# Three groups of loads move from SyncE's DMA queue to ScalarE's: the rows of the automaton, the gate's inputs, the gate's mix

## The chip, the cores and the metric

The kernel runs on one core of a Trainium2 chip. The metric is device time in microseconds, the median of several runs. One more execution was taken with the profiler; its own time stands beside its span in the table below. Engines are called as the profile calls them: PE (matrix multiplies), PEld (weight loads), DVE (vector), ACT (ScalarE), POOL (GpSimd), SP (SyncE, which only issues DMAs here). A "q" after an engine's name (SPq, ACTq) is its sequencer issuing a DMA.

## The reference, cut to what matters

The input x is 32 images of 8 channels, 256 x 256 pixels, f32. Layer 0 normalises x by groups of channels and adds to it a gated blend of two branches; layer 1 normalises again and adds a quantised 3x3 convolution.

```python
# layer 0, on n = groupnorm(x)
grid = n
for _ in range(15):                                  # branch 1: the lattice
    mapped = 3.9 * grid * (1 - grid)
    grid = 0.85 * (0.7 * mapped + 0.3 * conv3x3_depthwise(mapped)) + 0.15 * n
cml = clip(grid, 1e-4, 1 - 1e-4)
nca = sigmoid(conv1x1(relu(conv3x3(n, 8 -> 128)), 128 -> 8))      # branch 2: NCA
g = sigmoid(conv1x1(relu(conv3x3(concat(n, cml, nca), 24 -> 8)), 8 -> 8))   # the gate
x = x + g * cml + (1 - g) * nca
# layer 1
x = x + dequantised(conv3x3(quantised(groupnorm(x)), quantised(w))) + bias
```

## The kernel before

The program has a first stage that does all of layer 0 and the normalisation of layer 1, and a second stage for the quantised convolution. The change is in the first.

**Work of the first stage.** It goes through eight groups of four images. Four kinds of work are interleaved in one program:

- The lattice (`lattice`, `half`): for each group and channel, 15 steps, each in two halves of two images. A half is 32 multiplies (L502) into two of PE's result tiles, then on DVE two instructions `gt` (L513) and two that make the next state (L523). The states are `m_a` and `m_b`, two of each. Where a half writes `m_a`, `exchange` (L477, L478) issues two small DMAs on SP that copy rows of `m_a` between partitions; PE reads them in the next step of the same two images, which is two halves later. There are 896 exchanges. After every half `background` (L465) issues up to four more DMAs on SP from a list `later`: loads `d_a`, `d_b` of the next channel and stores of the finished one.
- NCA (`nca`): for each image eight tiles of 32 rows. `rows` (L569) loads the next tile into one of two buffers `im`, with 4 DMAs of 384 KB. A call of `hidden` is 12 multiplies from `im` (L588), then ACT's `h` (L596). There are eight calls to a tile, each followed later by four multiplies (L604) that sum into `acc`; after the tile, ACT's `nca` (L610).
- The gate (`gate`): again eight tiles to an image, one group behind NCA. `inputs` (L665) loads the next tile with 3 DMAs of 384 KB (two for `gin`, one for `gnc`; two buffers of each). PE's 80 multiplies L767 are followed by ACT's `r1` (L773), PE's L717 and ACT's `gate` (L719). `blend` (L675) loads `mix` with 2 DMAs of 384 KB into a single buffer, which ACT's `f` (L688) and POOL's `d` (L690) and `f` (L692) read; the next `mix` can be loaded only when these are done.
- Normalising the next group (`normalise`): loads `xr` (L306), ACT's `xq` (L370), stores (L336, L346).

**Order.** PE's order is the order of the program, written out by hand: `together` runs the lattice and lets out other work between its halves. For the other engines the planner of the framework sets the order in which their instructions are issued; each engine then issues its instructions in that order, and one that waits holds up those behind it.

**PE's result tiles.** `unit()` hands out three tiles `pt` in turn: a half takes two, a `hidden` one, a gate tile one. The multiplies that open a tile wait until its contents of three turns ago have been read, which for a `hidden` is ACT's `h`.

**DMA semaphores.** In the trace every DMA that SP or ACT issues counts on one of eight semaphores (100 to 104, 106 to 108), taken in turn across both queues, and it is issued only when the DMA that last used the semaphore has landed. SP's DMAs run on queue 1, ACT's on queue 10. In the first stage ACT issues none after its first 24 stores of zeros. In the second stage ACT issues 28 loads `yb` (L928) and 192 stores (L1001).

The lines of the loads, before the change:

```python
im = ims[(NT8 * b + t) % 2]
for k in range(2):
    for q in range(2):
        nc.sync.dma_start(im.bitcast(F32)[64 * q : 64 * q + 48, k, :, 1 : 1 + W], ...)   # L569
...
for j, to in enumerate((gin[:48], gin[48:], gnc)):
    nc.sync.dma_start(to, ...)                                                          # L665
...
for k in range(2):
    nc.sync.dma_start(mix[:, :, k, :], ...)                                             # L675
```

Of the kernel before, what the change touches and what calls it, by code (L numbers as in the profile page):

```python
# [109 lines left out]
def kernel(  # L110
# [15 lines left out]
    nc = tc.nc  # L126
# [3 lines left out]
    def dram_ap(t, offset, dims):  # L130
        return bass.AP(t.tensor, t.offset + offset, dims)
# [123 lines left out]
    with ExitStack() as one:  # L255
# [308 lines left out]
        def rows(b, t):  # L564

            im = ims[(NT8 * b + t) % 2]
            for k in range(2):
                for q in range(2):
                    nc.sync.dma_start(  # L569
                        im.bitcast(F32)[64 * q : 64 * q + 48, k, :, 1 : 1 + W],  # L570
                        dram_ap(
                            xp_s[b % NBUF], (32 * t + 16 * k + 8 * q) * ROW, [[W, 48], [ROW, 8], [1, W]]
                        ),
                    )
            return im
# [3 lines left out]
        def nca(b):  # L579
# [21 lines left out]
            def drain():  # L601
# [6 lines left out]
                if i == 3:  # L608
# [13 lines left out]
                    )  # L622

            ahead = loaded.pop(b, None) or rows(b, 0)
            for t in range(NT8):
                im = ahead
                acc = ps_a.tile([P, 512], F32, name="acc", tag="acc")
                for i in range(4):
                    hs = {}
                    for n in (i, i + 4):  # L630
                        hs[n], hs[n + 8] = hidden([im[64 * q : 64 * q + 48, :, n, :] for q in range(2)])
                        if n == 0:
                            if t < NT8 - 1:
                                ahead = rows(b, t + 1)
                            elif all((b + 1, g) in ready for g in range(4)):
                                loaded[b + 1] = rows(b + 1, 0)
                        yield 1.4
                    if i == 2 and done:
                        nc.sync.dma_start(*done)
                        done = None  # L640
                    if pend:
                        done = drain() or done
                    pend = (acc, t, i, hs)
                    yield 0.9
# [14 lines left out]
        def inputs(b, t):  # L659

            src = gs_s[b % NBUF]
            gin = gip.tile([96, 8, W], F32, name="gin", tag="gin")
            gnc = gip.tile([48, 8, W], F32, name="gnc", tag="gnc")
            for j, to in enumerate((gin[:48], gin[48:], gnc)):
                nc.sync.dma_start(  # L665
                    to, dram_ap(src, j * PART + 32 * t * C * W, [[W, 48], [4 * C * W, 8], [1, W]])
                )
            return gin, gnc

        def blend(b, t):  # L670

            src = gs_s[b % NBUF]
            mix = gip.tile([P, 3, 2, W], F32, name="mix", tag="mix", bufs=1)
            for k in range(2):
                nc.sync.dma_start(  # L675
                    mix[:, :, k, :],
                    dram_ap(src, (32 * t + 16 * k + 1) * C * W, [[W, P], [PART, 3], [1, W]]),
                )
            return mix
# [17 lines left out]
        def begin_gate(b):  # L697
            return scales(b), (inputs(b, 0), blend(b, 0))
# [9 lines left out]
        def gate(b):  # L708
# [38 lines left out]
            for t in range(NT8 + 1):  # L747
# [7 lines left out]
                if t < NT8:  # L755
                    (gin, gnc), mix = ahead
                    if t < NT8 - 1:
                        now["ahead"] = [inputs(b, t + 1)]
                    elif (b + 1) % GB:
                        staged[b + 1] = [inputs(b + 1, 0)]  # L760
                    pa = two[:, 0, :]
                    three = pa.rearrange("p (k w) -> p k w", w=W)
                    for j, src in enumerate((gin, gnc)):
                        rows_ = src.shape[0]
                        for n, (dx, to, of) in enumerate(PARTS):
                            for i in range(4):
                                T.matmul(  # L767
                                    three[32 * i : 32 * i + 32, :, to],
                                    gw[:rows_, j, dx, :], src[:, i::4, of],
                                    start=(j == 0 and n == 0), stop=(j == 1 and n == len(PARTS) - 1),  # L770
                                )
                    r1 = wk.tile([P, 512], F32, name="r1", tag="r1", bufs=1)
                    S.activation(r1, pa, AF.Relu, bias=bv[:, 0:1])  # L773
                    now["r1"], now["t"], now["mix"] = r1, t, mix
# [8 lines left out]
                def blend_(now):  # L783
                    if now["t"] < NT8 - 1:
                        now["ahead"].append(blend(b, now["t"] + 1))
                    elif (b + 1) % GB:
                        staged[b + 1] = scales(b + 1), (*staged[b + 1], blend(b + 1, 0))
# [293 lines left out]
```

## Time and profile before

| what | value |
|---|---|
| median of 3 runs | 12246.84 us (12240.68 to 12266.93) |
| the profiled execution | 12231.09 us, span 12229.3 us |
| PE busy | 10809.9 us, 88% |
| DVE busy | 7826.2 us, 64% |
| ACT busy | 3791.0 us, 31% |
| POOL busy | 1577.2 us, 13% |
| DMA on queue 1 (SP) | 1651.64 MB, 66.0% of 16 engines' span |
| DMA on queue 10 (ACT) | 89.53 MB, 2.3% |
| from 1500 to 11300 us (lattice, NCA and gate together) | PE busy 9109 of 9800 us |
| from 11660 us (second stage) | PE busy 273 of 570 us |

How to read it: the profile lists groups of instructions by source line, with the engine's idle time just before them and what ended it. "PE pt L502 <- DMA m_a<-m_a" is PE idle before a lattice multiply until the exchange of `m_a` had landed. The granted clock (PEclk) is a share of TensorE's full speed. Issuing a DMA does not count as busy time of ACT or SP, but it takes the sequencer's time, and the trace has its duration. The two rows for stretches are sums over a view of the profile that gives each engine's busy time window by window.

### The profile page before, as it was taken

The numbers are of one execution on the slowest core, as the hardware profiler recorded it, in microseconds if no ns is written. First come the engines' busy times: TensorE is split into PE (matmuls) and PEld (weight loads), VectorE is DVE, ScalarE is ACT, GpSimd is POOL, SyncE is SP. The second block draws the span as 40 slices with busy tenths as digits, with TensorE's granted clock in tenths as the row PEclk, the third lists the DMA queues.
The fourth block names the chain that finished last, engine by engine and source line by source line (L and its number), as shares of the span: only waits on it lengthen the run. The fifth ranks groups of instructions, "written<-read, shape, count | busy, mean of one in ns | idle before, by whom it ended". The sixth has DMA issues, their size and how long they took to land. (4 is left out here: it accounts for less than half of the span.)

```text
span 12229.3 us, 289998 instructions
## 1 busy us (share of the span) xinstructions
PE 10809.9 (88%) x124192; PEld 6033.0 (49%) x124192; DVE 7826.2 (64%) x11376; ACT 3791.0 (31%) x4034; POOL 1577.2 (13%) x2242
## 2 busy tenths in 40 slices
PE   4888899999999999999999999999999999999854
PEld 2544555555555555555555555555555555554222
DVE  4655666666666666666666666666666666665377
ACT  2222233332333333333333333333333333332133
POOL 1000011111111111111111111111111111111200
PEclk7999999999999999999999999999999999999776
DMA  6545567766777667766776667777677666665988
GB/s 171 97 98 102 101 136 147 143 140 138 147 142 148 137 137 145 151 141 134 148 151 139 135 140 147 143 145 149 133 146 149 141 133 129 126 123 114 204 249 259
DMA packets 2473159, 1759.74 MB, mean 144 GB/s; under 512 B 1021280, under 2 KB 2442944, under 8 KB 2471744
## 3 DMA queue, kind: packets, MB, share of 16 engines
q1 hardware_dynamic: 2380096, 1651.64, 66.0%
q10 hardware_dynamic: 91776, 89.53, 2.3%
q8 instruction: 979, 16.04, 0.6%
q14 instruction: 308, 2.52, 0.1%
HBM read 1130.62 MB, written 473.89 MB: 131 GB/s over the span
## 5 line engine op out<-in xcount | busy, mean ns | idle before, releaser
L596 ACT ACTIVATE h<-pt,bp_sb 128x1024 f32<-128x1024 f32 x2048 | 2275.6, 1113 | 4947.7 <-PE pt L588 4944.3
L588 PE MATMUL pt<-im,wp_hi 48*128 48x512 f32 x12288 | 2631.8, 424 | 165.4 <-ACT h L596 116.6
L502 PE MATMUL pt<-m_a,lw 64*64 64x325 f32 (+1 forms) x30720 | 2299.3, 433 | 464.9 <-DMA m_a<-m_a 410.1
L513 DVE SCALAR_TENSOR_TENSOR gt<-pt,d_b 128x650 f32<-128x650 f32 (+1 forms) x1920 | 1463.5, 763 | 1945.0 <-PE pt L502 1931.7
L588 PE MATMUL pt<-im,wp_lo 48*128 48x512 f32 x12288 | 2442.5, 393 | 0.2 <-issue 0.2
L513 DVE SCALAR_TENSOR_TENSOR gt<-pt,d_a 128x640 f32<-128x640 f32 (+1 forms) x1920 | 1447.2, 754 | 1531.5 <-PE pt L502 1528.2
L502 PE MATMUL pt<-m_b,lw 64*64 64x320 f32 (+1 forms) x30720 | 2200.5, 417 | 118.1 <-DVE gt L513 82.1
L502 PEld LDWEIGHTS pt<-m_a,lw 64*64 64x64 f32 x30720 | 1316.6, 138 | 1193.2 <-issue 596.9
L588 PEld LDWEIGHTS pt<-im,wp_hi 48*128 48x128 f32 x12288 | 1163.6, 185 | 1275.4 <-issue 719.4
L502 PEld LDWEIGHTS pt<-m_b,lw 64*64 64x64 f32 x30720 | 1237.4, 134 | 858.4 <-issue 463.5
L523 DVE SCALAR_TENSOR_TENSOR m_a<-gt 128x640 f32<-128x640 f32 (+1 forms) x1792 | 1431.7, 799 | 58.6
L523 DVE SCALAR_TENSOR_TENSOR m_b<-gt 128x650 f32<-128x650 f32 (+1 forms) x1792 | 1384.6, 774 | 101.3 <-DVE gt L513 2.8
L528 POOL TENSOR_TENSOR m_b<-m_b,junk 128x36 f32<-128x36 f32 x896 | 243.8, 272 | 7994.9 <-DVE m_b L523 5672.1
L588 PEld LDWEIGHTS pt<-im,wp_lo 48*128 48x128 f32 x12288 | 1168.7, 186 | 201.7 <-issue 0.6
L604 PE MATMUL acc<-h,wu_z 128*32 128x512 f32 x8192 | 1107.7, 612 | 0.0
L767 PE MATMUL pt<-gin,gw 96*32 96x384 f32 (+2 forms) x10240 | 772.0, 450 | 201.3 <-ACT gate L719 178.0
L277 PE MATMUL mark<-qw 64*64 64x1 bf16 x5760 | 947.6, 165 | 0.0
L277 PEld LDWEIGHTS <-qw 64*64 64x64 bf16 x5760 | 632.4, 110 | 205.4 <-issue 9.8
L767 PE MATMUL pt<-gnc,gw 48*32 48x126 f32 (+2 forms) x10240 | 733.1, 429 | 0.0
L767 PEld LDWEIGHTS pt<-gin,gw 96*32 96x32 f32 x10240 | 313.8, 115 | 823.7 <-issue 425.2
L690 POOL TENSOR_TENSOR d<-mix 128x256 f32<-128x256 f32 x512 | 552.1, 1095 | 1240.8 <-DVE gate L725 840.1
L767 PEld LDWEIGHTS pt<-gnc,gw 48*32 48x32 f32 x10240 | 295.0, 108 | 420.8 <-issue 415.3
(110 smaller groups left out, 5939.0 us busy)
## 6 DMA issues: line engine op xcount, KB each, us to landing
im<-xp_s SPq DMA_DIRECT2D x1024, 384.0 KB
gin<-gs_s SPq DMA_DIRECT2D x512, 384.0 KB
mix<-gs_s SPq DMA_DIRECT2D x512, 384.0 KB
gnc<-gs_s SPq DMA_DIRECT2D x256, 384.0 KB
d_a<-gs_s SPq DMA_DIRECT2D x2048, 36.0 KB
yb<-y_s ACTq DMA_DIRECT2D x28, 2432.0 KB
xr<-in_x_dram SPq DMA_DIRECT2D x128, 512.0 KB
xp_s<-hi SPq DMA_DIRECT2D x256, 256.0 KB
```

The costliest lines, as they stand in the source:

```text
L277: T.matmul(one_[dst], qw[src, 0, dst], qw[src, 0, 0:1], start=True, stop=True)
L502: T.matmul(pt[dst], lw[src, c, w, dst], rhs[src], start=first, stop=not first)
L513: V.scalar_tensor_tensor(gt.rearrange("p (u c) -> p u c", u=2), pt[:, :, : w * n], FLOOR, d[:, ts, :].rearrange("p (u t) j -> p u (t j)", ...
L523: V.scalar_tensor_tensor(to, gt, 1.0, gt, ALU.subtract, ALU.mult)
L528: G.tensor_tensor(edge, edge, junk.unsqueeze(1).to_broadcast([P, TU, 2]), ALU.mult)
L588: T.matmul(ph[:, i, :].rearrange("p (h w) -> p h w", w=W), w[64 * i : 64 * i + 48, dx, :], rhs[:, :, dx : dx + W], start=(dx == 0 and w is ...
L596: S.activation(h.rearrange("p i c -> p (i c)"), ph.rearrange("p i c -> p (i c)"), AF.Relu, bias=bp_sb)
L604: T.matmul(acc[32 * g : 32 * g + 32], wu_z[:, 24 - 8 * i : 56 - 8 * i], hs[4 * g + i], start=(i == 0), stop=(i == 3),)
L690: G.tensor_tensor(d[:, cols], mix[:, 1, k], mix[:, 2, k], ALU.subtract)
L767: T.matmul(three[32 * i : 32 * i + 32, :, to], gw[:rows_, j, dx, :], src[:, i::4, of], start=(j == 0 and n == 0), stop=(j == 1 and n == le ...
```

## The change

The three `nc.sync.dma_start` in `rows`, `inputs` and `blend` become `nc.scalar.dma_start`. They stand at the same places of the program. In all 2304 DMAs of 384 KB go from SP's queue to ACT's: 1024 for `im`, 768 for `gin` and `gnc`, 512 for `mix`.

```diff
@@ def rows(b, t):
             for k in range(2):
                 for q in range(2):
-                    nc.sync.dma_start(
+                    nc.scalar.dma_start(
                         im.bitcast(F32)[64 * q : 64 * q + 48, k, :, 1 : 1 + W],
@@ def inputs(b, t):
             for j, to in enumerate((gin[:48], gin[48:], gnc)):
-                nc.sync.dma_start(
+                nc.scalar.dma_start(
                     to, dram_ap(src, j * PART + 32 * t * C * W, [[W, 48], [4 * C * W, 8], [1, W]])
@@ def blend(b, t):
             for k in range(2):
-                nc.sync.dma_start(
+                nc.scalar.dma_start(
                     mix[:, :, k, :],
```

## The prediction

> **What bounds the kernel now.** I read the page first, then busy time by windows, then who waited for whom on PE, then single stretches of the timeline. From 1500 to 11300 us every window looks like this one (PE, PEld, DVE, ACT, POOL busy, then clock and DMA share):
>
> ```profile
> 2000.00:4000.00 2000.00, 1854.78 (x21940) 1041.44 (x21938) 1314.59 (x1963) 637.74 (x664) 287.63 (x394) 0.98 0.71 143
> ```
>
> PE is busy 93% and its order is fixed, so the first stage lasts as long as PE's work plus PE's waits. ACT is busy 32%. The longest of PE's waits in the whole run (us in total, times, longest):
>
> ```profile
> PE pt L502 <- DMA m_a<-m_a: 410.1, 153, 12.3
> PE pt L990 <- ACT ob L995: 235.6, 28, 12.8
> PE pt L767 <- ACT gate L719: 178.0, 218, 0.9
> PE pt L588 <- ACT h L596: 116.6, 84, 2.1
> ```
>
> The first is the exchange of `m_a`, an SP DMA. One case in the timeline shows why it is late:
>
> ```profile
> 2612.25 1.93 SPq L569 DMA_DIRECT2D im<-xp_s  x4
> ...
> 2614.63 0.62 SPq L477 DMA_DIRECT2D m_a<-m_a  x1
> ...
> 2615.29 0.60 SPq L478 DMA_DIRECT2D m_a<-m_a  x1
> ...
> 2626.57 1.79 PE L502 MATMUL pt<-m_a,lw 64*64 64x325 f32 x11 [8.08 <-DMA m_a<-m_a]
> ```
>
> The exchange was issued in time, but four `im` loads (1.5 MB) were ahead of it on queue 1, and it landed after them: PE waited 8.08 us. From the trace's DMA packets I worked out, for each exchange, the time from the end of L478's issue to its last packet (2112 bytes; nothing else has that size), and how many 1 KB packets queue 1 started meanwhile. The usual value is 1.0 us. In 348 exchanges over 200 such packets went first, up to 1411, and the median is then 5.4 us in the first group and 2.8 later. These 348 carry 390 of PE's 410 us. In the longest cases the packets are those of `im`, `gin` and `mix`, the transfers that move.
>
> A long wait costs twice. In the window behind this one the granted clock is 0.50:
>
> ```profile
> 2626.00:2628.00 2.00, 1.43 (x13) 0.93 (x17) 0.00 (x0) 0.00 (x0) 0.00 (x0) 0.50 1.13 342
> ```
>
> The first 11 multiplies took 1.79 us; the same group, with a warm clock, took 0.99 at 2613.64. In all PE worked 229 us at half clock next to waits for `m_a` (300 to 11300 us), half of which, 114 us, is lost.
>
> **What the change removes.** 2304 DMAs leave SP and queue 1. Two things come of it.
>
> (a) SP's time. Their issues take 521 (`im`, mean 0.509), 439 (`gin`, `gnc`, mean 0.572) and 254 us (`mix`, mean 0.496) on SP, 1.21 ms. I cost this at nothing: SP waited 3298 us for DVE to write `m_a`, and the median exchange was issued 0.06 us after that. The cover is missing in 77 exchanges issued over 0.5 us late; 87 of the 89 us that PE waited for these belong to the 348 and are counted below.
>
> (b) The queue. How soon an exchange lands when the big loads run on queue 10 beside it the first stage doesn't show. From below: as in an empty queue, 1.0 us, extra 0. From above the nearest row is the second stage, where SP's stores run beside ACT's 2.4 MB load on queue 10. A store of 112 KB lands 2.44 us after its issue when few packets of queue 10 are under way and 4.78 (median) when over 200 are: extra 2.3 us, though the load itself takes 11 to 13 us. So the other queue does not have to drain first. I put the extra latency on the 348 and compare with the moment PE wanted the data (its start less its wait): left-over waits are 33 us at 0.5, 64 at 1.0, 126 at 1.5, 248 at 2.3. I take 1.5, as an exchange has one or two packets to a DMA engine where the store has seven. Gain in waits 390 - 126 = 264; of the 114 lost to the clock some 80, since the long waits go first. Together 345 us; bounds 142 + 40 = 182 and 357 + 114 = 471.
>
> The Trainium skill speaks against this: "DMA: Bandwidth & Descriptors", section "Issuing engines are not separate DMA queues", says that DMAs of all issuers run on the same 16 engines and interleave, and that spreading them saves only issue time, by which the gain would be that of (a), nothing. The same page, section "Queues, rings and completion order", has each engine take turns between queues by packets of some 9 to 17 descriptors, which at the 46 ns of one 1 KB packet in queue 10 is an estimate of 0.4 to 0.8 us extra and a gain near 440.
>
> **What it adds: ACT issues them.** The cost of one on ACT: the second stage has the same kind on both queues, L1001 at a median of 812 ns on SP and 823 on ACT, so SP's durations can be used:
>
> ```profile
> L569 SPq DMA_DIRECT2D im<-xp_s x1024: 302/463/2093, 174.4 to 11197.1; - x171
> L665 SPq DMA_DIRECT2D gin<-gs_s x512: 302/470/1907, 1504.8 to 11639.7; - x171
> L665 SPq DMA_DIRECT2D gnc<-gs_s x256: 302/470/3036, 1505.4 to 11640.4; - x128
> L675 SPq DMA_DIRECT2D mix<-gs_s x512: 358/472/2002, 1585.7 to 11648.2; - x171
> ```
>
> Four for `im` hold ACT 2.0 to 2.6 us, three for the gate 1.5, two for `mix` 1.0. Behind them waits above all `h`, which gives PE its result tile back. ACT in the same stretch as above:
>
> ```profile
> 2609.88 1.11 ACT L596 ACTIVATE h<-pt,bp_sb 128x1024 f32<-128x1024 f32 x1 [3.12 <-PE pt L588]
> 2613.64 1.11 ACT L596 ACTIVATE h<-pt,bp_sb 128x1024 f32<-128x1024 f32 x1 [2.65 <-PE pt L588]
> 2616.96 0.69 ACT L610 ACTIVATE nca<-acc,bv 128x512 f32<-128x512 f32 x1 [2.21 <-PE acc L604]
> ```
>
> The gap ahead of an `h` is 2.65 us or more here, and after it PE needs the tile a median of 0.86 us later (0.05 at the 10th percentile, 1.87 at the 75th; worked out from the three-tile turn). So the bare issues fit. I laid a block of given length into ACT's timeline, pushed what follows, and counted what exceeds the slack of each `h` and `gate`. For the 256 sets of `im`: placed after the last `h` of the tile before, 5 us at a length of 2.1, 43 at 4, 377 at 6; placed after the next `h`, 39, 290 and 716. Gate loads: 0 to 27 us at 1.45, 3 to 96 at 3. `mix`: 0 to 10 at 0.95, 3 to 117 at some 3.
>
> The length is what is unknown, as ACT also takes over three waits.
> - *The buffer.* `im` waits for PE's last read, which the `h` ahead has waited for: nothing. `gin` likewise. `mix` waits for POOL, now SP's wait; with it ACT is held 2.6 us after `f`, 3 us of loss in all by the count above:
>
> ```profile
> SPq L675 <- POOL f L692: 92.4, 78, 1.6
> ```
>
> - *The data*, stored a group earlier: nothing but in the first image.
> - *The semaphore turn.* Each DMA waits until the one eight before it has landed, on either queue. With the order of before and SP's landings, ACT would stand 2.2 us more on average if it came to `im` right after the last `h` of the tile before (loss 215 us), 0.7 if four more DMAs lay between (36), and 0.06 if after the next `h` (36 us, mostly the issues).
>
> The sum of `im` is thus 5 to 377 us; I take 100, between 36 and 215. For the gate's loads 35 (0 to 96), for `mix` 15 (0 to 117). Loss 150. Elsewhere nothing: the second stage is unchanged, and the gates at the end (11300 to 11660 us) have their loads issued where ACT has 70.84 us of work in 360.
>
> **Sum.** 345 - 150 = 195 us off the profiled execution's 12231.09 (span 12229.3): 12036. The median of the runs lies 15.75 higher, so 12052.
>
> **Rivals.**
> - *The queue frees everything and ACT hides all* (the 471 less some 45): about 12247 - 430 = 11820. For it: 2.65 us gaps. Against it: DMA engines are 70% busy, so an exchange meets traffic in any queue.
> - *PE's next wait takes the place.* The 153 waits vanish, but PE then waits for DVE's `gt` (96.4 us now) or for `h`; gain and loss cancel: 12247.
> - *No gain from a queue of its own*; only ACT's 150 remain, 12247 + 130 = 12375, slower. Against it: the 2.44 to 4.78 us above.
> - *ACT stuck in the semaphore turn: slower.* In the second stage ACT already stands still behind its own issues:
>
> ```profile
> ACT ob L995 <- DMA out_dram<-ob: 310.6, 31, 14.2
> ```
>
>   If each set of `im` holds ACT 6 us rather than 3, the loss is 377 to 716 us, mean 546, against a gain of 345: 12247 + 200 = 12447. It decides from a hold of about 5.5 us. For it: `im` lands 8.6 us (median) after issue and four of them take half the turn. Against it: SP's own wait in L569 is short (mean 0.509, median 0.463).
>
> That the change does something else is open in one way: the planner, not the text, places these issues among ACT's instructions; that is the spread between the two placements.
>
> **Chances.** Forecast 0.53, everything hidden 0.12, the wash 0.08, no gain from the queue 0.09, ACT stuck 0.18. A measurement can tell about 0.2% (24 us) from no change. Faster 0.53 + 0.12 = 0.65, same 0.08, slower 0.27. The range 11860 to 12400 leaves out some 0.07 below and 0.10 above.
>
> **What would show it.** Right: PE's wait for `m_a` falls from 410 us to about 150, most exchanges land within 1 to 2.5 us of L478, the clock's 0.98 rises towards 1.00; PE's wait for `h` grows by 100 to 200 us. Wrong: waits for `m_a` stay (queue), or PE's waits for `h` and `gate` grow by 400 us and ACT's `h` is released by DMAs instead of PE (turn).

## The result and the profile after

The changed kernel takes 13112.5 us (median of 4 runs, 13101.84 to 13130.85) against 12243.76 for before: a ratio of 1.0709, 95% interval 1.0688 to 1.073. It is 869 us slower. The forecast was 195 us faster, and the range ended at 12400.

The profiled execution of after has a span of 13110.2 us. The window that opened the prediction now reads (same columns: PE, PEld, DVE, ACT, POOL busy, clock, DMA share, GB/s):

```profile
2000.00:4000.00 2000.00, 1749.70 (x19932) 977.24 (x19928) 1189.93 (x1788) 575.11 (x599) 260.80 (x362) 0.94 0.64 130
```

PE does 9% fewer multiplies in the same 2 ms (19932, not 21940), is busy 105 us less, and its granted clock is 0.94 in place of 0.98. The longest waits of PE (us in total, times, longest), now:

```profile
PE pt L502 <- DMA m_a<-m_a: 665.2, 236, 11.2
PE pt L767 <- ACT gate L719: 282.1, 224, 12.0
...
PE pt L588 <- ACT h L596: 164.1, 92, 6.3
PE pt L502 <- DVE gt L513: 156.8, 114, 5.9
```

The wait for the exchange, which the change was to shorten to about 150 us, has grown from 410 to 665. The timeline shows how it looks on a queue of its own:

```profile
5604.77 0.31 ACTq L569 DMA_DIRECT2D im<-xp_s  x1
...
5605.20 1.06 ACTq L569 DMA_DIRECT2D im<-xp_s  x2
...
5605.27 0.60 SPq L477 DMA_DIRECT2D m_a<-m_a  x1
...
5605.92 0.60 SPq L478 DMA_DIRECT2D m_a<-m_a  x1
...
5616.04 1.36 PE L502 MATMUL pt<-m_a,lw 64*64 64x325 f32 x8 [6.51 <-DMA m_a<-m_a]
```

Three `im` loads went out on ACT's queue in the half microsecond before the exchange's issue and during it; the exchange's 32 packets were alone on their queue up to PE's start, and PE still waited 6.51 us for them.

Where the 881 us between the two profiled spans (12229.3 and 13110.2) lie, from the trace:

| | before | after | difference |
|---|---|---|---|
| to the last lattice multiply, PE idle | 1053 | 1576 | +522 |
| the same, PE busy | 10219 | 10538 | +319 |
| of that, PE busy at half clock | 460 | 1100 | +641 |
| the last gates | 386 | 423 | +37 |
| second stage | 571 | 574 | +3 |

Work at half clock takes twice its time, so 641 us more of it are 320 us lost: this is all of the growth of PE's busy time. The clock went with the waits: where PE stood idle longer, it also worked longer at half clock. In PE's idle time up to the second stage, summed over lines, the exchange grew by 255 us (410 to 665), DVE's `gt` by 140 (121 to 261), ACT's `gate` by 104 (178 to 282), ACT's `h` by 65 (158 to 223).

One more line of after does not come from the queue. DVE waited 64.2 us for the input of the normalisation before; after, the line reads

```profile
DVE stats L318 <- DMA xr<-in_x_dram: 459.6, 107, 9.9
```

No `xr` load was moved. But the planner, which orders every engine except PE, has answered the moved DMAs with a new order for DVE, SP, POOL and ACT; in it DVE stands still at the statistics until `xr` is there, with `gt` behind. With DVE kept in the old order this wait is 54.0 us (after_dve_old below).

### The profile page after: what moved, and what is told of

Read it like the earlier page. It is cut to its first block, busy times and chain, and to the rows that moved or that the text cites. A ratio compares the mean times of both kernels' runs of the same rounds, so it can differ in the third digit from the quotient of the medians.

```text
span 13110.2 us, 288494 instructions
## 1 busy us (share of the span) xinstructions
PE 11143.5 (85%) x124192; PEld 6182.0 (47%) x124192; DVE 7805.1 (60%) x11376; ACT 3783.5 (29%) x4034; POOL 1562.2 (12%) x2242
## 5 line engine op out<-in xcount | busy, mean ns | idle before, releaser
L502 PE MATMUL pt<-m_a,lw 64*64 64x325 f32 (+1 forms) x30720 | 2468.8, 458 | 784.8 <-DMA m_a<-m_a 665.2
L588 PE MATMUL pt<-im,wp_hi 48*128 48x512 f32 x12288 | 2659.9, 429 | 261.3 <-ACT h L596 164.1
L502 PE MATMUL pt<-m_b,lw 64*64 64x320 f32 (+1 forms) x30720 | 2227.9, 422 | 139.5 <-DVE gt L513 84.1
L502 PEld LDWEIGHTS pt<-m_a,lw 64*64 64x64 f32 x30720 | 1412.0, 145 | 1568.7 <-issue 887.1
L767 PE MATMUL pt<-gin,gw 96*32 96x384 f32 (+2 forms) x10240 | 820.1, 472 | 282.1 <-ACT gate L719 282.1
L767 PE MATMUL pt<-gnc,gw 48*32 48x384 f32 (+2 forms) x10240 | 753.1, 439 | 0.0
```

What stands on the lines that cost most here:

```text
L502: T.matmul(pt[dst], lw[src, c, w, dst], rhs[src], start=first, stop=not first)
L588: T.matmul(ph[:, i, :].rearrange("p (h w) -> p h w", w=W), w[64 * i : 64 * i + 48, dx, :], rhs[:, :, dx : dx + W], start=(dx == 0 and w is ...
L767: T.matmul(three[32 * i : 32 * i + 32, :, to], gw[:rows_, j, dx, :], src[:, i::4, of], start=(j == 0 and n == 0), stop=(j == 1 and n == le ...
```

## The experiments

Three theories. **Shared engines**: both queues feed the same DMA engines, so a load of 384 KB ahead of the exchange holds it up on whichever queue it is, and on another queue even a load that is issued after it can. **ACT held**: the issues and waits that ACT took over delay `h` and `gate`. **New order**: what counts is the planner's other order. To part the last from the others, some kernels keep the order of another kernel: edges without any wait, from each instruction of an engine to the next in the first stage, bind the planner (`keep_order`); the loads in question are left free unless it is said otherwise. Each group of kernels was timed beside its own runs of before, with medians of 12251 to 12275 us; differences are to those.

### Which loads, and how much is the order

```diff
# act_old_order: after, with DVE, POOL, SP and ACT's other work in the order of before
-        nc.sync.dma_start(...)        # L569, L665, L675
+        nc.scalar.dma_start(...)
+    keep_order(tc)                    # before's order
# sp_new_order: before (loads on SP), the other work in the order of after
+    keep_order(tc)                    # after's order
# only_rows: L569 alone on nc.scalar;  only_gin: L665 alone on nc.scalar; planner free
```

act_old_order. 

> The moved loads stay on ACT's queue, but DVE, POOL, SP's other DMAs and ACT's activations are bound to the order that the planner gave them in the kernel before; only the places of the moved loads among ACT's instructions are left to the planner. Theory 'new order' (the loss comes from the order that the planner gave the other engines once SP was relieved): 12200 to 12400 us, PE's clock back at 0.97 or more in the steady part. Theory 'ACT held' (the loss comes from ACT's issues and its waits for DMA semaphores): 12850 to 13150 us, as in the changed kernel. The prediction's sum, 345 us of gain from a queue of its own less 150 of hold, would give some 12050 once the order is out of the way.

sp_new_order. 

> The reverse: all loads on SP's queue as before, but DVE, POOL, ACT's activations and SP's other DMAs are bound to the order of the changed kernel; the places of the 2304 loads among SP's DMAs are left to the planner. 'New order': 12800 to 13100 us. 'ACT held': 12230 to 12400 us. PE's waits for the exchange of m_a tell the same: 600 us or more against about 400.

only_rows. 

> Only the 1024 loads of im go to ACT's queue, free order. 'ACT held': im is the largest block (four issues, 2 us) and nearly half of all issues, so 300 to 500 us of the 870 are to be seen, 12550 to 12750. 'New order': the loss follows the planner, not the number of loads; any value from 12200 to 13100, with DVE's wait for xr (460 us in the changed kernel, 64 before) going along with it.

only_gin. 

> Only the 768 loads of gin and gnc go to ACT's queue, free order. 'ACT held': up to 100 us, as the issues follow an activation after which ACT has some 5 us: 12250 to 12350. 'New order': not bound to the number of loads, 12200 to 13100, together with DVE's wait for xr.

| kernel | us | ratio, interval | PE's wait for `m_a` | at half clock, lattice |
|---|---|---|---|---|
| act_old_order | 12794.55 | 1.044, 1.0424 to 1.0457 | 670 | 815 |
| sp_new_order | 13881.27 | 1.133, 1.1312 to 1.1347 | 1153 | 1244 |
| only_rows | 12962.4 | 1.0578, 1.0557 to 1.0599 | 579 | 934 |
| only_gin | 12370.43 | 1.0095, 1.008 to 1.011 | 379 | 555 |

With before's order 543 us of the loss stay, more than the new-order theory allowed and less than the other; some 326 come with the new order (869 less 543). With the loads on SP the new order is worse still (13881, above both expectations), so what an order costs depends on the queues. The rows of NCA are the main part: alone they cost 711 us, in an order of the planner's own, and the gate's loads 119.

In act_old_order the exchange's wait is already as long as in after. I worked out from the trace's packets how long each exchange took to land, from the end of L478's issue to the last of its 32 packets, by the number of `im`, gate and `mix` loads issued in the 4 us before L477 (in brackets, how many exchanges):

| loads | 0 | 1 | 2 | 3 | 4 |
|---|---|---|---|---|---|
| before (one queue), mean us | 1.50 (733) | 3.72 (25) | 3.08 (66) | 5.97 (29) | 8.16 (43) |
| after (two queues), mean us | 1.34 (657) | 3.62 (112) | 4.58 (101) | 6.38 (23) | 4.77 (2) |

A queue of its own did not help: over all 896 exchanges the mean is 2.14 us in before and 2.13 in after. The second queue also allows what one queue rules out, that a load is issued while SP is still issuing the exchange (some 1.3 us). With none in the 8 us before, this happened to 55 exchanges of after; they landed after 2.86 us in the mean, and PE waited 46 of its 665 us for them. Loads issued in the microsecond behind the exchange's issue did no harm: 1.09 us in after (54 exchanges), 1.12 in before (125).

### Packets, issues, or semaphores

```diff
# rows_act_old: im alone on ACT, every engine in the order of before
-                    nc.sync.dma_start(im...)
+                    nc.scalar.dma_start(im...)
# rows_act_old_small: the same, one of eight rows to a load (the others stay zero)
-   im...[64 * q : 64 * q + 48, k, :, 1 : 1 + W],   ... [[W, 48], [ROW, 8], [1, W]]
+   im...[64 * q : 64 * q + 48, k, 0:1, 1 : 1 + W], ... [[W, 48], [ROW, 1], [1, W]]
# rows_sp_old_small: the same small loads on nc.sync, in before's places
# rows_pool_old: im alone and whole on nc.gpsimd
```

rows_act_old. 

> Only NCA's rows (im) go to ScalarE's queue; gate inputs and mix stay on SP's, and every engine keeps the order of before. The shared-engines theory (packets of the second queue reach the DMA engines while an exchange is under way, also those issued after it) expects most of the 545 us that all three loads cost in the old order, since im's are 40 of the 49 loads or so of a band: 12,600 to 12,750 us, the exchange's wait on PE 550 to 650 us. The ACT-held theory expects the same total by another way: exchange wait near 410 us, and PE's waits for ACT (h, evictions) 100 us or more above before. The new-order theory expects 12,250 to 12,300 us, since the order is the old one.

rows_act_old_small. 

> As rows_act_old, but each of im's loads fetches one of its eight rows (7/8 of what NCA's first layer reads of the state is left at zero), so that the number of DMAs, their places and their semaphores stay, and the packets are an eighth. To be read beside its twin on SP's queue. Shared-engines theory: within 100 us of the twin, and the exchange's wait on PE below 250 us in both. ACT-held theory: the 300 to 450 us between ScalarE's queue and SP's stay, since each load is issued as before and takes its turn among the semaphores as before.

rows_sp_old_small. 

> The twin: all loads on SP's queue in the order of before, im's loads cut to one of eight rows (7/8 of what NCA's first layer reads is left at zero). If the exchange waits because im's packets are ahead of it in the queue, its wait on PE falls from 410 to below 200 us and the time to 11,900 to 12,050 us; if the loads' number counts and not their packets, 12,200 us or more.

rows_pool_old. 

> Only im's loads, whole, on GpSimd's queue, every engine in the order of before; GpSimd's DMAs do not share the eight semaphores of SP and ScalarE. In rows_act_old the late issue on SP stood for 203 us of PE's 704 us of exchange waits, the landing for 327. If the turn of the semaphores made SP late, that part falls below 50 us and the time to 12,450 to 12,600 us; if the late issue is only slow landings seen from another side, the time stays at 12,650 to 12,800 us. That GpSimd's own work (the edges of m_b, d for the mix) then stands behind loads that wait is a cost of its own, 0 to 200 us.

rows_act_old took 12743.11 us (1.0393, 1.0377 to 1.041), 477 more than before. The small pair took 11838.84 (0.9652) on ACT and 11796.44 (0.9615) on SP: 42 us apart, where the whole loads are 477 apart. The number of DMAs, their places and their semaphores are the same in both; only the packets are an eighth. PE's wait for the exchange in rows_act_old:

```profile
PE pt L502 <- DMA m_a<-m_a: 721.1, 159, 14.7
```

In rows_act_old_small:

```profile
PE pt L502 <- DMA m_a<-m_a: 82.2, 58, 4.6
```

In rows_sp_old_small, with the loads on SP:

```profile
PE pt L502 <- DMA m_a<-m_a: 70.6, 54, 3.3
```

So the bare issuing of `im` by ACT costs some 40 us, and the packets cost the rest, directly or, as will be seen, through the semaphores that they hold longer. The small pair also shows what the exchange's delay is worth in before: without it 470 us less.

In rows_act_old the exchange lands sooner than in before (1.67 us in the mean, not 2.14), but SP issues it late: 0.91 us after DVE has written `m_a`, 0.20 in before. SP's own waits say why (of rows_act_old; the line reads 294.0 us in before):

```profile
SPq L465 <- DMA im<-xp_s: 647.4, 221, 10.9
```

L465 is a small DMA for the lattice. It needs nothing of `im`; it needs the semaphore that an `im` load of ACT's queue, eight DMAs earlier, has not given back. The exchange stands behind it. On POOL's queue `im` doesn't share those semaphores (its DMAs count on 111 to 118): rows_pool_old took 12571.75 us (1.0255, 1.0227 to 1.0283), SP was late by 0.19 us, the landing was back at 2.16, and

```profile
PE pt L502 <- DMA m_a<-m_a: 593.5, 178, 9.7
```

The turn of the semaphores is worth about 166 us (477 less 311), as far as POOL's own cost of issuing can be neglected; the other 311 us stay with either second queue.

Why they stay the means don't tell: in rows_pool_old an exchange is issued and lands as soon as in before (0.19 and 2.16 us against 0.20 and 2.14), yet PE waits 183 us more. What differs is which exchanges are late. PE does the same work in the same order in these kernels, so I sorted the exchanges by the time that PE leaves them: from the end of L478's issue to the end of PE's work ahead of the half that reads the rows, taken from rows_sp_old_small, where little disturbs it. In each cell: mean landing in us, exchanges that land after more than 4 us, PE's wait in us.

| PE leaves | under 3 us (328 exchanges) | 3 to 5 us (282) | over 5 us (286) |
|---|---|---|---|
| before | 2.15; 39; 347 | 1.50; 13; 38 | 2.76; 72; 25 |
| rows_pool_old | 2.29; 50; 365 | 2.24; 43; 199 | 1.93; 30; 29 |
| after | 2.30; 63; 412 | 2.45; 56; 210 | 1.62; 21; 43 |

With the loads on SP the delays fell mostly on exchanges that PE needs late, where they cost little; sent from another queue, about as many exchanges are delayed, and more of them are ones that it needs sooner. Of `im`'s loads, 409 went out within 8 us ahead of an exchange of the last kind in before and 45 ahead of one of the middle kind; in rows_pool_old it is 205 and 118. Of the 124 exchanges that took over 4 us in before only 17 do so in rows_pool_old and 11 in after. The 183 us and the 321 us more of work at half clock that came with them (160 us lost) are about the 344 us between the profiled spans of rows_pool_old and before.

### The exchange by itself

```diff
# landing: only this, 12 times over for each case; when = before or behind, queue = SP, ACT or POOL
+        if when == "before":
+            touch(); rows(queue, 4); V.memset(pause[:, 0:512], 0.0)
+        V.memset(m_a[:, :, 1 : 1 + NJ], 0.0)
+        exchange(m_a)
+        if when == "behind":
+            touch(); rows(queue, 4)
+        V.tensor_copy(seen[:, 0:36], m_a[:, :, 1:3])      # L170
```

`touch` writes a column of `im`, so that the loads wait for DVE as the exchange does.

> The kernel's work is left out (the output is filled with zeros); what is left is the exchange alone, twelve times in each of seven cases: with no load near it; with four of im's loads issued about a microsecond before it, on SP's queue, on ScalarE's or on GpSimd's; and with the four issued just behind it, on each of the three. Measured is the time from the end of the second exchange DMA's issue to the landing of the exchange's last packet. Shared-engines theory: alone 1.0 us; loads before it 5 to 8 us on whichever queue; loads behind it 1.0 to 1.2 us on SP's queue, 2 us or more on the two others. If a queue of its own frees the exchange as the prediction had it: 2.5 us or less behind loads on ScalarE's queue, and no more than 1.5 us with loads issued after it.

From the end of the second exchange DMA's issue to its last packet, median of 12:

| loads | none | 4 before, SP | before, ACT | before, POOL | 4 behind, SP | behind, ACT | behind, POOL |
|---|---|---|---|---|---|---|---|
| us | 0.99 | 8.71 | 8.99 | 9.38 | 1.04 | 5.30 | 2.95 |

The first pass through the seven cases, as the instruction that reads `m_a` waits for it (in the order of the table; the bracket is its wait):

```profile
15.91 0.18 DVE L170 COPY seen<-m_a 128x36 f32<-128x36 f32 x1 [2.87 <-DMA m_a<-m_a]
...
32.58 0.18 DVE L170 COPY seen<-m_a 128x36 f32<-128x36 f32 x1 [10.88 <-DMA m_a<-m_a]
...
50.05 0.18 DVE L170 COPY seen<-m_a 128x36 f32<-128x36 f32 x1 [11.67 <-DMA m_a<-m_a]
...
67.97 0.18 DVE L170 COPY seen<-m_a 128x36 f32<-128x36 f32 x1 [12.12 <-DMA m_a<-m_a]
...
75.88 0.18 DVE L170 COPY seen<-m_a 128x36 f32<-128x36 f32 x1 [2.71 <-DMA m_a<-m_a]
...
100.50 0.18 DVE L170 COPY seen<-m_a 128x36 f32<-128x36 f32 x1 [8.05 <-DMA m_a<-m_a]
...
115.63 0.18 DVE L170 COPY seen<-m_a 128x36 f32<-128x36 f32 x1 [5.79 <-DMA m_a<-m_a]
```

Loads that are ahead hold the exchange up by some 8 us on all three queues: the queue makes little difference. With the loads on ACT the exchange's first packet starts a median of 8.7 us after its issue began, while the last `im` packet lands at 9.7: it goes through almost at the end of the loads, not among them. Behind POOL's loads its first packet starts at 4.5 us and its last at 10.4. That the loads hold it up is shown; whether they do so in the DMA engines, or ahead of them where packets are handed out, these runs don't tell apart. Loads behind it on SP's queue do nothing; on ACT's they cost 4.3 us. This is a matter of time: SP can issue them only when it is done with the exchange (1.4 us after its start), ACT started at 0.06 us, so that its first packet (1.02 us) came ahead of the exchange's own (1.25 us when alone). Loads that ACT issues only after the exchange's issue were not tried here; in after they did no harm (1.09 us, above). The Trainium skill's "DMA: Bandwidth & Descriptors", section "Issuing engines are not separate DMA queues", has it that all issuers share the same engines and that spreading DMAs saves only issue time; 8.71 against 8.99 us agrees.

### What the order costs

```diff
# after_small: after, in after's full order, im's loads of one row
# act_old_small: act_old_order, im's loads of one row
# after_dve_old, after_dve_sp_old, after_dve_act_old: after, with
+    keep_order(tc)      # before's order, for DVE; DVE and SP; DVE and ACT's activations
```

after_small. 

> All three loads on ScalarE's queue in the full order of after, im's loads cut to one of eight rows (7/8 of what NCA's first layer reads is left at zero). Its twin is rows_sp_old_small, 11,796 us. If after's order costs by the transfers that it puts side by side, 11,800 to 11,950 us; if the order costs by itself (VectorE's statistics waiting for xr, stores late on SP), the 320 us between after and act_old_order stay: 12,050 to 12,200 us.

act_old_small. 

> All three loads on ScalarE's queue, every engine in the order of before, im's loads cut to one of eight rows (7/8 of what NCA's first layer reads is left at zero). It stands between rows_act_old_small (11,839: im alone on ScalarE's queue) and after_small (12,424: all three, in after's order). If the 585 us between them come from the order: 11,850 to 11,950 us. If they come from the whole gate inputs and mix rows that share the engines with the exchange from a second queue: 12,250 to 12,400 us. PE's wait for the exchange says the same, below 120 us or above 250.

after_dve_old. 

> All three loads on ScalarE's queue, VectorE kept in the order of before, the other engines ordered anew by the planner. Beside after (13,112) and act_old_order (12,795). If VectorE's place for the statistics (460 us of waiting for xr in after) is what the new order costs: 12,750 to 12,900 us. If it is where the other transfers and the loads land: 13,000 us or more.

after_dve_sp_old. 

> All three loads on ScalarE's queue; VectorE and SP kept in the order of before, GpSimd and ScalarE ordered anew. VectorE alone took 117 us off after (12,996); all four engines take 318 off (12,795). If SP's order of stores, fetches and exchanges is the missing 200 us: 12,780 to 12,860 us; if it is ScalarE's places for the loads among its evictions: 12,950 us or more.

after_dve_act_old. 

> All three loads on ScalarE's queue; VectorE and ScalarE's activations kept in the order of before, SP and GpSimd ordered anew. The other half of after_dve_sp_old: 12,780 to 12,860 us if ScalarE's order is the missing 200 us, 12,950 us or more if it is SP's.

after_small took 12424.04 us (1.0122, 1.0094 to 1.0151), act_old_small 12063.94 (0.9837, 0.9819 to 0.9854). The order is worth 360 us with `im`'s packets gone and some 320 with them there (13112.5 less 12794.55): it costs by itself, and "by the transfers side by side" falls. Both kernels lie outside the ranges given: after_small above the higher, act_old_small between the two. The other 225 us between act_old_small and rows_act_old_small are the gate's loads and `mix` on the second queue; beside whole `im` loads the same two add only 66 (543 less 477), so the delays overlap. PE's wait for the exchange in after_small:

```profile
PE pt L502 <- DMA m_a<-m_a: 340.1, 121, 8.2
```

And in act_old_small:

```profile
PE pt L502 <- DMA m_a<-m_a: 215.5, 109, 4.5
```

after_dve_old took 12995.66 us (1.0595, 1.0575 to 1.0615). DVE's wait for `xr` is gone and PE's wait for `gt` back from 261 to 126 us, but the gate is as late as in after:

```profile
PE pt L767 <- ACT gate L719: 294.3, 224, 12.6
```

So DVE's order is 117 of the 320, a time between the two expectations. With SP's order too it is 12772.12 (1.041, 1.0395 to 1.0426); with ACT's in place of SP's 12764.39 (1.0407, 1.0383 to 1.043). Either takes back all of the rest, and the two expectations, which gave it to one or the other, both fall. That the planner fits these orders to each other, so that binding one engine binds the next, would explain it, but is not shown. Which single instruction of the new order costs the last 200 us stays open.

### The other direction: one queue, loads behind the exchange

If loads behind an exchange are harmless on one queue, the loads can stay on SP and be sent just after the second of two neighbouring exchanges.

```diff
# after_pair: L569, L665, L675 put their loads in a list, which is sent
+            for _ in range(min(n, len(bulk))):
+                tc.keep_in_program_order(nc.sync.dma_start(*bulk.pop(0)))
# after the second exchange of a pair
+                    if s == 0:
+                        send(5)
# and in full ahead of each tile of NCA or of the gate; after_pair2: only what the tile needs;
# pair_7, pair_9: after_pair2 with send(7), send(9)
```

after_pair. 

> All loads on SP's queue, whole, but kept back and sent, at most five at a time, just after the second of two neighbouring groups' exchanges, so that they have the longest free stretch before the next exchange. Shared-engines theory: loads issued behind an exchange on the same queue do not delay it (landing 1.14 us in before), so PE's wait for the exchange falls from 410 us to below 200 and the time to 11,850 to 12,100 us. ACT-held theory: says nothing of it, since no load is on ScalarE's queue. New-order theory: the planner is given other positions, and any time from 12,000 to 13,000 us could follow; above 12,400 us with an exchange wait below 200 us would be its sign.

after_pair2. 

> As after_pair, all loads whole on SP's queue, but a consumer sends only the loads that it needs itself. In after_pair 90 of the gate's tiles sent four waiting im loads early, most of them into the four microseconds between the two exchanges of a pair, and about five waits of 6 us in each millisecond followed from these. Shared-engines theory: with these gone PE's wait for the exchange falls from 357 us to below 200, the time PE works at half clock in the lattice from 541 to 450 us or less, and the time to 11,900 to 12,100 us. If the loads' places do not matter in one queue: 12,250 us as after_pair. The planner again orders the other engines anew, which has cost up to 360 us elsewhere.

pair_7. 

> after_pair2 with up to seven loads in each long gap in place of five. In after_pair2 the exchange's wait fell to 140 us, but PE waited 530 us for gin and 468 for im, with up to nine loads in the list and five sent. If the loads were late because five are too few: these two waits fall to a third, the exchange's wait stays below 250 us (seven loads take some 15 us, the long gap has a median near 17), and the time is 12,000 to 12,300 us. If they are late because every load now waits for an exchange at all: 13,000 us or more.

pair_9. 

> The same with up to nine loads, that is, always the whole list. Waits for gin and im as in before (23 and 18 us) or little above; the exchange's wait back to 200 to 400 us, since nine loads take some 19 us and reach into the next exchange; 12,000 to 12,300 us.

| kernel | us | ratio, interval | PE's waits: `m_a` | `gin` |
|---|---|---|---|---|
| after_pair | 12249.24 | 0.9988, 0.9978 to 0.9998 | 357 | 44 |
| after_pair2 | 13769.95 | 1.1233, 1.121 to 1.1256 | 140 | 530 |
| pair_7 | 12722.55 | 1.0372, 1.0346 to 1.0397 | 583 | 149 |
| pair_9 | 12642.15 | 1.0307, 1.0286 to 1.0329 | 605 | 148 |

after_pair is no different from before by the 0.2% bound; its gate tiles sent waiting `im` loads into the gap between two neighbouring exchanges, as the text on after_pair2 tells. In after_pair2 the mechanism shows: the exchanges land in 1.08 us in the mean, and PE's wait for them, the last line below, is down from 410. The loads are late instead:

```profile
PE pt L786 <- DMA gin<-gs_s: 530.0, 85, 14.6
PE pt L601 <- DMA im<-xp_s: 467.9, 131, 18.9
...
PE pt L511 <- DMA m_a<-m_a: 140.1, 76, 6.5
```

With seven or nine at a time the exchange still lands in time (1.2 us in pair_9), yet PE waits for it, since SP issues it 1.4 us late in the mean. SP's small DMAs stand in the turn behind a block of loads (pair_9):

```profile
SPq L474 <- DMA im<-xp_s: 533.1, 328, 3.7
```

The wait for `gin` did fall to less than a third, as expected, but the exchange's did not stay low, and both kernels took longer than the 12,300 us expected at most: sent in larger blocks, the loads bring the wait back as a late issue. No place that I tried for the loads beats before; that none can is not shown.

## Why the prediction was wrong, point by point

- *What bounds the kernel* was right: PE and its waits, the exchange first, each wait paid again in clock. Cutting `im`'s packets on SP takes 470 us off, beside the 410 and 114 us that the prediction counted for all loads. Its 348 delayed exchanges are too many: counted by 32 packets to an exchange, 270 had over 200 packets of 1 KB ahead. These carry 378 of the 410 us, so the reading holds.
- *(a) SP's time is worth nothing*: nothing contradicts it. SP was relieved of 2304 issues and the exchange was issued later, not earlier (0.31 us after DVE in the mean, 0.20 in before).
- *(b) The queue: this is the step that failed.* I took 1.5 us of extra latency for an exchange on a queue beside the loads, with 2.3 as the upper end. It is 8.0 us behind four loads (8.99 less 0.99), nearly the same as in one queue, and in after the mean landing is 2.13 us against 2.14: the gain of 345 us is zero. And the extra was put on the same 348 exchanges, as if the loads kept their places ahead of these; but the exchanges that land late are others (11 of 124 the same), and PE needs them sooner. The bound of 2.3 us came from stores of the second stage beside a load on ACT's queue; "the nearest row" had other sizes and another load, and why it was milder was not tried. The page of the Trainium skill that spoke against the change was named and then overruled by that row. The estimate of 0.4 to 0.8 us, from the turns by packets in the section "Queues, rings and completion order" of the same page, is not borne out by the 8.0 us either.
- *The bound of zero gain was too kind.* I had "no gain from a queue of its own" as the worst case of (b), at 12375 us (with 130 us for ACT, not the sum's 150). With `im` on POOL's queue the loss is 311 us: the delays moved to exchanges that PE needs sooner (its wait for those with 3 to 5 us left rose from 38 to 199 us). Loads issued during an exchange's issue, from which one queue keeps it safe, are the smaller part: 31 of PE's 594 us in rows_pool_old, 46 of 665 in after. Nothing in the prediction asked what the common queue protects.
- *ACT's hold, 150 us*: too much in itself. With small loads on ACT it is 42 us for `im`, where I took 100. The slack counted ahead of `h` was there. SP's durations were also too long for ACT: an `im` load's issue has a median of 310 ns on ACT in after, 463 on SP in before.
- *The semaphore turn*: it was seen, but looked for on ACT. It is SP that is caught, and with it the exchange: about 166 us. The rival "ACT stuck in the turn" had the sign and the mechanism, and the wrong engine.
- *What was missing*: that the planner reorders all other engines. The prediction mentioned only the places of the moved issues among ACT's instructions; the order is worth some 320 us, 117 of it by DVE's place for its statistics.

Summed from the experiments: `im` on a second queue 311, the shared turn 166, the other two loads 66, the order 326: 869 us, by construction the whole, as each is the step from one kernel to the next.

The signs that the prediction named did tell it: "waits for `m_a` stay (queue)" came, and worse; the clock fell instead of rising.

## What to carry to other kernels

In these kernels a small, urgent DMA is held up by the large transfers issued ahead of it, whichever queue they are on; moving them to another queue removes nothing ahead of it. It gives up what the common queue did unseen: no load could go out during the small one's issue, and the loads mostly went out ahead of exchanges that PE needed late. A mean landing time does not show this; one has to ask which transfer is late, and how soon it is needed. Before moving a DMA, ask what its present place in the queue keeps away, who shares its semaphores, and whether a planner will reorder engines that the change doesn't touch; a kernel with the old order kept tells this last part at once. Taking away bytes near the urgent transfer gained 4% here (in a kernel that leaves out seven eighths of NCA's input), where no way that I tried of moving them gained anything.

## What the runs showed of the hardware that was not expected

- Four loads of 384 KB ahead of an exchange of 32 packets delay it from 0.99 to 8.71, 8.99 and 9.38 us on SP's, ACT's and POOL's queue: in these cases a second queue brought no turn-taking that helps the small one.
- Loads that start on another queue while the exchange is being issued delay it by 4.3 us (ACT) and 2.0 us (POOL); in after, loads that ACT issued in the microsecond behind the exchange's issue did not (1.09 us).
- Waits cost more than half as much again in clock: in the lattice, 522 us more idle time came with 641 us more work at half clock, that is 320 us.
